# A graph layer with a residual and a norm: how the gathers of the prologue are held back

## The chip, the cores and the metric

One core of one Trainium2 chip runs the whole program. The metric is the device time of one execution in microseconds (us). Times are given as the median of several timed runs; a profile is one further execution, with a time of its own. TensorE is the matrix engine (PE in the profile, its weight loads PEld), VectorE is DVE, ScalarE is ACT, GpSimd is POOL, and SyncE (SP) issues most DMAs. GpSimd issues the indirect DMAs (the gathers) in this kernel.

## What is computed

A graph attention layer over N = 6250 nodes of 64 features and 206,250 edges sorted by destination, four heads of 16, with a residual and a layer norm:

```python
Qh = (x @ Wq.T + bq).reshape(n, H, D)
Kh = (x @ Wk.T + bk).reshape(n, H, D)
Vh = (x @ Wv.T + bv).reshape(n, H, D)
Ee = (edge_attr @ We.T + be).reshape(-1, H, D)
...
score = (Kh[src] * Qh[dst] * (1.0 / np.sqrt(D)) * Ee).sum(-1)
score = jnp.exp(jnp.clip(score, -5.0, 5.0))
msg = Vh[src] * score[..., None]
wV = jax.ops.segment_sum(msg, dst, num_segments=n)
...
x = _layernorm(x + wV.reshape(n, H * D))
```

So each edge needs k and v of its source node, q of its destination, and its own edge values; messages are summed by destination.

## The kernel before

The edges are cut into tiles of 128 and groups of G = 8 tiles (202 groups). Two groups make a step, except for the last eight groups, which are steps of their own. k and v of a step's sources lie in one of five buffers `kvs`, step s in `kvs[s % 5]`.

The prologue (lines 259 to 534) makes two tables in DRAM, `kv_tab` with k and v of every node and `q3_tab` with q cut into three bf16 parts. The loop of line 416 runs over five chunks of ten blocks of 128 nodes; TensorE multiplies two blocks at a time (line 424, a pair of products in one PSUM tile, 25 pairs), ScalarE copies k and v out (line 426) and takes the first part of q, VectorE the rest, and SyncE writes each chunk to the tables (lines 454 and 456). Between the pairs VectorE also works out masks, keys and the least destination of each group. SyncE then reads key rows, sources and edge values back for the first groups of the main part (lines 473 to 479).

Gathers from `kv_tab` cannot begin before the table is written. So the first two steps (groups 0 to 3, 32 tiles) get their k and v another way: GpSimd gathers rows of x itself, which is an input (line 318, `collect`), into the last of the five buffers, one gather a tile, 128 rows. Later TensorE turns them (`x_turned`, line 481), ScalarE copies the turned tiles, TensorE multiplies by the weights of k and v (line 494) and VectorE adds the bias and writes k and v into `kvs[0]` and `kvs[1]` (line 496). This goes by half groups, the eight entries of `order`; the loop of line 514 does one each time, and the turning of the next one is issued ahead of the product of this one. Between them stand ScalarE's and VectorE's pieces of work on x in three bf16 parts (`parts_of_x`) and ScalarE's one-hot rows (`onehot_rows`).

Steps 2 and 3 (groups 4 to 7) are the first whose k and v come from `kv_tab`. Their gathers are the eight lots of `lots(2) + lots(3)`, four gathers each, three in the last two (two tiles of every odd group from 7 on are picked by TensorE instead). `gather` (line 252) issues a lot.

Every engine works through its instructions in the order of the program. `behind` adds a wait by hand: a gather issued with it starts only when the named instruction is done. `mark` is a list of TensorE's instructions to wait for; before, these are the products of the tables and the first products of k and v. Nothing else orders GpSimd in the prologue except the data: src_x for gathers of x, the written `kv_tab` and src_i for those of k and v, and readers of a buffer that is overwritten.

Before, 8 gathers of x are issued at once and six lots of 4 follow in the loop of line 416, at the pairs 1, 4, 7, 10, 13 and 16; the first gather of each lot waits for the newest product. In the loop of line 514 each lot of steps 2 and 3 waits for the product of the same round:

```python
            first_kv(*gh, xe)
            xe = following
            gather(((lots(2) + lots(3))[i], mark[-1]))
```

The main part (from line 546, in a branch on a number that the prologue works out) loops over the 202 groups. In each, TensorE selects queries and node rows with one-hot matrices, turns terms and sums messages; VectorE makes the products (line 666), scores and messages; GpSimd issues the gathers of four steps ahead, each lot behind a TensorE instruction named in `where`.

Of the kernel before, what the change touches and what calls it, by code (L numbers as in the profile page):

```python
# [14 lines left out]
P = 128  # L15
N = 6250
C = 64
# [4 lines left out]
G = 8  # L22
# [18 lines left out]
XG = 4  # L41
# [63 lines left out]
def tile_gnn(ctx: ExitStack, tc: tile.TileContext, x, xT, wT, bias, beT, weT, eT, src, src_rows, dst,  # L105
             dst_rows, out):
    nc = tc.nc
# [48 lines left out]
    wkv = consts.tile([P, 2, 2 * C], F32, name="wkv")  # L156
# [102 lines left out]
    with tc.tile_pool(name="nodes", bufs=1) as nodes, \  # L259
# [49 lines left out]

        x_rows = kvs[KVB - 1].rearrange("p t (u c) -> p (t u) c", u=2)  # L310
        XS = [x_rows[:, g * G:(g + 1) * G, :] for g in range(XG)]
        first_lots = [(g, range(j, j + G // 2)) for g in range(XG) for j in (0, G // 2)]
        mark = []

        def collect(lot):
            g, js = lot
            for j in js:
                ins = nc.gpsimd.indirect_dma_start(
                    out=XS[g][:, j, :], out_offset=None, in_=x[:, :],
                    in_offset=bass.IndirectOffsetOnAxis(ap=src_x[:, g * G + j:g * G + j + 1], axis=0))  # L320
                if mark and j == js[0]:
                    behind(ins, mark[-1])

        collect(first_lots[0])
        collect(first_lots[1])


        nc.vector.tensor_scalar(ident, diff, 0.0, None, op0=OP.is_equal)
# [87 lines left out]
        for i in range(NB // CB):  # L416
            bs = slice(i * CB, (i + 1) * CB)
            kv_sb = chunks.tile([P, CB, 2 * C], F32, name="kv_sb")
            for b in range(0, CB, 2):
                two = slice(i * CB + b, i * CB + b + 2)  # L420
                ps = npsum.tile([P, 2, 3 * C], F32, name="ps")
                for u in range(2):
                    c0 = (i * CB + b + u) * P
                    mark.append(nc.tensor.matmul(ps[:, u, :], xT_sb[:, c0:c0 + P], w_sb, start=True,  # L424
                                                 stop=True))
                nc.scalar.activation(kv_sb[:, b:b + 2, :], ps[:, :, :2 * C], AF.Copy)
                q = ps[:, :, 2 * C:]
                nc.scalar.activation(q3[:, two, 0], q, AF.Copy)
                nc.vector.tensor_sub(q, q, q3[:, two, 0])
                late.append((q, two))  # L430
                if len(late) > 1:
                    rest_of_q()
                place = i, b
                if place == (0, 4):
                    for some in x_nodes:
                        nc.vector.memset(some[3 * P // 4:], 0.0)
                if place == (2, 0):
                    three_parts(be_p, be_sb, C, G)
                if place == (2, 4):
                    nc.vector.tensor_reduce(most, rows_i, axis=AX.X, op=OP.max)  # L440
                if place == (2, 8):
                    nc.vector.tensor_reduce(least, rows_i, axis=AX.X, op=OP.min)
                if place == (3, 0):
                    weights()
                if place == (3, 4):
                    three_parts(bkv_p, bkv_sb, 2 * C, 2)
                if place == (3, 8):
                    wide, one = destinations()
                if place == (4, 4):
                    masks()  # L450
                pair = (i * CB + b) // 2
                if pair % 3 == 1 and pair // 3 + 2 < len(first_lots):
                    collect(first_lots[pair // 3 + 2])
            nc.sync.dma_start(kv_v[:, bs, :], kv_sb)
            if i:
                nc.sync.dma_start(q3_v[:, bs.start - CB:bs.start], q3[:, bs.start - CB:bs.start])
            if i == 0:
                nc.sync.dma_start(rows_i, dst_rows)
            if i == 1:
                nc.sync.dma_start(src_i, src)  # L460
                nc.sync.dma_start(x_nodes[0][:N // NB], by_rows[:, :30 * C])
            if i == 2:
                nc.sync.dma_start(x_nodes[1][:N // NB], by_rows[:, 30 * C:])
                nc.sync.dma_start(dst_i, dst)
# [26 lines left out]
        def first_kv(g, h, xe):  # L491
            pv = npsum.tile([P, 4, 2 * C], F32, name="pv", bufs=2)
            for u in range(2):
                mark.append(nc.tensor.matmul(pv[:, 2 * u:2 * u + 2, :], xe[:, u, :], wkv, start=True,
                                             stop=True))
            nc.vector.tensor_add(kv_of(g)[:, 4 * h:4 * h + 4, :], pv,
                                 bkv_all[:, None, :].to_broadcast([P, 4, 2 * C]))

        def parts_of_x(i, part):

# [12 lines left out]
            parts_of_x(k, 0)  # L513
        for i, gh in enumerate(order):
            following = x_turned(*order[i + 1]) if i + 1 < len(order) else None
            first_kv(*gh, xe)
            xe = following
            gather(((lots(2) + lots(3))[i], mark[-1]))
            if i < 3:
                parts_of_x(i, 1)  # L520
                parts_of_x(i, 2)
# [7 lines left out]
            if i % 2:  # L529
                onehot_rows(i // 2, early_to[i // 2])  # L530
                onehot_rows_rest(i // 2)
        for b in range(RING):
            nc.sync.dma_start(acc[:, b, :], x[b * P:(b + 1) * P, :])
        later.close()
# [537 lines left out]
```

## Time and profile before

| | us |
|---|---|
| median of 3 timed runs | 2184.07 |
| lowest and highest of them | 2179.05, 2185.28 |
| profiled execution, its own time | 2166.65 |
| span of its profile | 2164.4 |
| busy in it: TensorE | 1896.9 |
| VectorE | 1212.6 |
| ScalarE | 881.3 |
| GpSimd | 1354.4 |

A row of the timeline has the start, the length, the engine, the line, the operation, output and inputs, and the shape; in brackets stands how long the engine had been idle and what ended that by the profile. Neighbouring instructions of one line and tile are merged, with their count behind an x. A tile is named by its buffer, so the gathers of x, which go into a `kvs` buffer, show as `kv<-in_x,src_x` and those of k and v as `kv<-kv_tab,src_i`. "issue" and "remote" are idle times that no event in the profile explains. A q behind an engine's name means its sequencer. Ends of matrix products are modelled, and some of their records can be missing.

### The profile page before, as it was taken

How to read it: one execution, taken by the hardware profiler on the slowest of the kernel's cores; microseconds unless marked ns; L12 is line 12 of the kernel's file. 1: busy time of each engine (PE TensorE's matmuls, PEld its weight loads, DVE VectorE, ACT ScalarE, POOL GpSimd, SP SyncE). 2: the span in 40 equal slices, each digit the busy share in tenths (PEclk: the TensorE clock that was granted, in tenths of full speed). 3: DMA queues.
4: the chain of work that ended last, by engine and by line, in shares of the span. 5: the costliest groups of instructions: out<-in, count | busy, mean ns of one | idle time of the engine just before them, and what ended most of it. 6: DMA issues, size and time to landing. Idle time of an engine off the chain costs nothing.

```text
span 2164.4 us, 26225 instructions
## 1 busy us (share of the span) xinstructions
PE 1896.9 (88%) x9156; PEld 1116.6 (52%) x9156; DVE 1212.6 (56%) x2179; ACT 881.3 (41%) x1166; POOL 1354.4 (63%) x1426
## 2 busy tenths in 40 slices
PE   6489999899888989899889889889898889989996
PEld 5245555455454555455455455555554545545555
DVE  6356556555555465665555555565655655655664
ACT  3343443443443434434434434434444344344343
POOL 5556666666666666666666666666666666666441
PEclk9688889888999889889989988988999988988995
DMA  6533343443343334434334433433433333333231
GB/s 179 185 96 92 108 110 96 112 110 97 111 114 92 105 98 118 113 97 114 106 96 115 111 90 110 116 90 110 113 103 111 97 110 110 95 111 109 83 90 25
DMA packets 141160, 230.01 MB, mean 106 GB/s; under 512 B 71056, under 2 KB 71506, under 8 KB 140906
## 3 DMA queue, kind: packets, MB, share of 16 engines
q1 hardware_dynamic: 95322, 135.39, 21.3%
q0 software_dynamic: 45312, 91.84, 16.8%
q8 instruction: 74, 1.21, 0.2%
q10 hardware_dynamic: 384, 1.00, 0.2%
q14 instruction: 68, 0.56, 0.1%
HBM read 220.31 MB, written 7.79 MB: 105 GB/s over the span
## 4 chain that ended last, share of the span: by engine, by line
PE 79%; issue 12%; DVE 3%; ACT 3%; another core or an unknown queue 2%; DMA 1%; SPq 0%; DVEq 0%; POOL 0%; ACTq 0%
PE pick L621 37%; PE room L621 24%; PE ee L621 11%; PE qe L650 4%; PE qq L621 3%; ACT off L693 1%; ACT to L224 1%; ACT to L218 1%; PE ps L424 1%; DMA kb<-key_tab 0%; ACT eb L632 0%; DVE hot L585 0%; DVE prod L666 0%; DVE score L669 0%
## 5 line engine op out<-in xcount | busy, mean ns | idle before, releaser
L235 POOL DMA_INDIRECT kv<-kv_tab,src_i x1384 | 1322.7, 956 | 750.3 <-issue 359.5
L621 PE MATMUL pick<-hot,parts 128*128 128x512 bf16 x3675 | 911.7, 405 | 16.3 <-issue 15.5
L621 PEld LDWEIGHTS <-parts 128*128 128x128 bf16 x3675 | 383.1, 105 | 561.8 <-issue 225.5
L645 DVE TENSOR_TENSOR term<-eb,qq 128x512 f32<-128x512 f32 x202 | 138.2, 684 | 757.3 <-remote 201.2
L621 PE MATMUL room<-msg,off 128*128 128x64 f32 x3192 | 462.3, 306 | 72.3 <-issue 69.6
L621 PEld LDWEIGHTS room<-msg,off 128*128 128x128 f32 x3192 | 438.6, 220 | 103.1 <-issue 99.9
L585 DVE TENSOR_TENSOR hot<-from,still 128x1536 bf16<-128x1536 bf16 (+1 forms) x384 | 375.7, 978 | 0.0
L621 PE MATMUL ee<-et,we_sb 128*128 128x512 f32 x404 | 274.1, 765 | 114.0 <-issue 86.1
L616 ACT ACTIVATE kv<-room 128x256 f32<-128x256 f32 x98 | 37.7, 384 | 819.3 <-DVE acc L719 542.9
L224 ACT ACTIVATE to<-to,one_p 126x1024 bf16<-126x1024 bf16 x198 | 226.9, 1146 | 6.4
L218 ACT ACTIVATE to<-kb,minus_row 126x1024 bf16<-126x1024 bf16 x198 | 224.8, 1135 | 0.0
L693 ACT ACTIVATE off<-of 128x2048 f32<-128x2048 bf16 (+2 forms) x105 | 191.5, 1825 | 6.9 <-DVE of L658 6.9
L675 ACT ACTIVATE score<-score 128x32 f32<-128x32 f32 x202 | 44.7, 221 | 357.9 <-DVE score L671 190.4
L632 ACT ACTIVATE eb<-ee,be_col 128x512 f32<-128x512 f32 x202 | 135.1, 669 | 29.5 <-DMA kb<-key_tab 22.4
L621 PEld LDWEIGHTS ee<-et,we_sb 128*128 128x128 f32 x404 | 73.9, 228 | 141.0 <-issue 108.2
L682 DVE TENSOR_TENSOR msg<-kv,score 128x512 f32<-128x512 f32 x202 | 137.8, 682 | 8.4 <-PE room L621 7.4
L669 DVE TENSOR_REDUCE score<-prod 128x32 f32<-128x512 f32 x202 | 138.3, 684 | 7.0
L666 DVE TENSOR_TENSOR prod<-kv,qe 128x512 f32<-128x512 f32 x202 | 137.2, 679 | 6.4 <-ACT kv L616 1.4
L658 DVE TENSOR_TENSOR of<-still,key 128x2048 bf16<-128x2048 bf16 (+2 forms) x105 | 123.1, 1173 | 7.0 <-ACT off L693 6.5
L650 PE MATMUL qe<-ident,term 128*128 128x128 f32 x806 | 123.3, 276 | 4.2 <-DVE term L645 2.1
L650 PEld LDWEIGHTS qe<-ident,term 128*128 128x128 f32 x806 | 101.9, 143 | 44.1 <-issue 3.7
L719 DVE SCALAR_TENSOR_TENSOR acc<-room,above,acc 128x64 f32<-128x64 f32 x101 | 28.5, 283 | 97.3 <-PE room L621 28.6
(124 smaller groups left out, 758.9 us busy)
## 6 DMA issues: line engine op xcount, KB each, us to landing
et<-in_eT SPq DMA_DIRECT2D x100, 512.0 KB
kb<-key_tab SPq DMA_DIRECT2D x201, 252.0 KB
kv<-kv_tab,src_i POOLq DMA_INDIRECT x1384
srcs<-in_src_rows SPq DMA_DIRECT2D x49, 256.0 KB
qw<-q_tab SPq DMA_DIRECT2D x202, 15.8 KB
kv_tab<-kv_sb SPq DMA_DIRECT2D x5, 640.0 KB
q_tab<-q SPq DMA_DIRECT2D x5, 480.0 KB
acc<-in_x SPq DMA_DIRECT2D x48, 32.0 KB
```

The source lines that it names most:

```text
L218: nc.scalar.activation(TO[g][:, :n, :], KB.pop(g)[:, :n * P].rearrange("p (j e) -> p j e", j=n), AF.Square, bias=minus_row3[:3 * W])
L224: nc.scalar.activation(TO[g][:, :n, :], TO[g][:, :n, :], AF.Relu, bias=one_p[:3 * W], scale=-1.0)
L235: return nc.gpsimd.indirect_dma_start(out=kv_of(g)[:, j, :], out_offset=None, in_=kv_tab[:, :], in_offset=bass.IndirectOffsetOnAxis(ap=src ...
L585: nc.vector.tensor_tensor(HOT[m, c][:, :hi - lo].rearrange("p b (a c) -> p b a c", c=2), pairs(FROM[m])[:, None].to_broadcast(shape), bloc ...
L621: mark.append(nc.tensor.matmul(*aps, **kw))
L632: nc.scalar.activation(EB[g][:, :n], ee[:, :n], AF.Identity, bias=be_col)
L645: nc.vector.tensor_mul(TERM[g][:, :n], EB.pop(g)[:, :n], qq[:, :n])
L650: nc.tensor.transpose(qe[g % 2][:, 2 * u:2 * u + 2, :].rearrange("p j c -> p (j c)"), TERM[g][:, u, :], ident)
L666: nc.vector.tensor_mul(prod[:, :n, :], kv_of(g)[:, :n, :C], qe[g % 2][:, :n, :])
L669: nc.vector.tensor_reduce(score, prod[:, :n, :].rearrange("p g (h d) -> p g h d", h=H), axis=AX.X, op=OP.add)
L682: nc.vector.tensor_mul(MSG[s][:, k:k + n, :].rearrange("p g (h d) -> p g h d", h=H), kv_of(g)[:, :n, C:].rearrange("p g (h d) -> p g h d", ...
L693: nc.scalar.activation(OF[s][:, :n, :], OH.pop(s)[:, :n, :], AF.Copy)
```

## The change

The gathers of x after the first eight are no longer issued in lots. `collect` issues one gather, and from the first pair of table products on, each pair is followed by one gather that waits for that pair's newest product, until all 32 are out (24 gathers, pairs 0 to 23). In the loop of the first k and v, `first_kv` no longer appends its products to `mark` but returns VectorE's addition, and a lot of steps 2 and 3 waits for that addition. The lots come one round later: in round i, from 1 on, lot i - 1 is issued behind addition i, and the last lot after the loop, behind addition 7 as well.

```diff
-        first_lots = [(g, range(j, j + G // 2)) for g in range(XG) for j in (0, G // 2)]
+        first_tiles = [(g, j) for g in range(XG) for j in range(G)]
         mark = []
 
-        def collect(lot):
-            g, js = lot
-            for j in js:
-                ins = nc.gpsimd.indirect_dma_start(
-                    out=XS[g][:, j, :], out_offset=None, in_=x[:, :],
-                    in_offset=bass.IndirectOffsetOnAxis(ap=src_x[:, g * G + j:g * G + j + 1], axis=0))
-                if mark and j == js[0]:
-                    behind(ins, mark[-1])
-
-        collect(first_lots[0])
-        collect(first_lots[1])
+        def collect(g, j):
+            ins = nc.gpsimd.indirect_dma_start(
+                out=XS[g][:, j, :], out_offset=None, in_=x[:, :],
+                in_offset=bass.IndirectOffsetOnAxis(ap=src_x[:, g * G + j:g * G + j + 1], axis=0))
+            if mark:
+                behind(ins, mark[-1])
+
+        for _ in range(G):
+            collect(*first_tiles.pop(0))
...
                 pair = (i * CB + b) // 2
-                if pair % 3 == 1 and pair // 3 + 2 < len(first_lots):
-                    collect(first_lots[pair // 3 + 2])
+                if first_tiles:
+                    collect(*first_tiles.pop(0))
...
             for u in range(2):
-                mark.append(nc.tensor.matmul(pv[:, 2 * u:2 * u + 2, :], xe[:, u, :], wkv, start=True,
-                                             stop=True))
-            nc.vector.tensor_add(kv_of(g)[:, 4 * h:4 * h + 4, :], pv,
-                                 bkv_all[:, None, :].to_broadcast([P, 4, 2 * C]))
+                nc.tensor.matmul(pv[:, 2 * u:2 * u + 2, :], xe[:, u, :], wkv, start=True, stop=True)
+            return nc.vector.tensor_add(kv_of(g)[:, 4 * h:4 * h + 4, :], pv,
+                                        bkv_all[:, None, :].to_broadcast([P, 4, 2 * C]))
...
-            first_kv(*gh, xe)
+            added = first_kv(*gh, xe)
             xe = following
-            gather(((lots(2) + lots(3))[i], mark[-1]))
+            if i:
+                gather(((lots(2) + lots(3))[i - 1], added))
...
+        gather(((lots(2) + lots(3))[-1], added))
         for b in range(RING):
```

## The prediction, on record before the changed kernel ran

> **What bounds the kernel now.** I read the page first: its span and the chain of work that ended last, by engine.
>
> ```profile
> span 2164.4 us, 26225 instructions
> ...
> PE 79%; issue 12%; DVE 3%; ACT 3%; another core or an unknown queue 2%; DMA 1%; SPq 0%; DVEq 0%; POOL 0%; ACTq 0%
> ```
>
> TensorE holds 79% of the chain and GpSimd 0% of it. The change edits GpSimd gathers of the prologue alone, so it can act only through who waits for them, or through the DMA engines. Next I read the group of the main loop's first VectorE product (one a group of edges), which shows how long the loop lasts.
>
> ```profile
> L666 DVE TENSOR_TENSOR prod<-kv,qe x202: 413/679/689, 112.5 to 2151.0; 128x512 f32<-128x512 f32 x101
> ```
>
> It comes 202 times between 112.5 and 2151.0 us: (2151.0 - 112.5) / 201 = 10.14 us a group. So about 112 us are prologue and entry, the part that the change can move; the loop behind it is not edited. Third, the timeline of the prologue's end: VectorE's additions 1 to 7 of the first k and v (numbered from 0), TensorE's last product for them, and TensorE's first instruction of the main part.
>
> ```profile
> 62.54 0.68 DVE L496 TENSOR_TENSOR kv<-pv,bkv_all 128x512 f32<-128x512 f32 x1
> 63.87 0.68 DVE L496 TENSOR_TENSOR kv<-pv,bkv_all 128x512 f32<-128x512 f32 x1
> ...
> 71.38 0.69 DVE L496 TENSOR_TENSOR kv<-pv,bkv_all 128x512 f32<-128x512 f32 x1 [0.69 <-issue]
> ...
> 75.37 0.67 DVE L496 TENSOR_TENSOR kv<-pv,bkv_all 128x512 f32<-128x512 f32 x1
> ...
> 79.70 0.68 DVE L496 TENSOR_TENSOR kv<-pv,bkv_all 128x512 f32<-128x512 f32 x1
> ...
> 81.74 2.08 PE L494 MATMUL pv<-wkv,xe 128*128 128x256 f32 x4 [0.41 <-ACT xe L488]
> ...
> 90.16 0.69 DVE L496 TENSOR_TENSOR kv<-pv,bkv_all 128x512 f32<-128x512 f32 x1 [9.78 <-remote]
> 99.25 0.69 DVE L496 TENSOR_TENSOR kv<-pv,bkv_all 128x512 f32<-128x512 f32 x1 [8.40 <-remote]
> 100.00 0.10 PEld L556 LDWEIGHTS <-row_b 128*128 128x128 bf16 x1 [16.91 <-DVE kv L496]
> ```
>
> The last addition ends at 99.25 + 0.69 = 99.94 and the main part starts at 100.00: this addition, not a gather, ends the prologue. Its product is on record as done at 81.74 + 2.08 = 83.82, so the last two additions came 8.4 to 9.8 us later than the recorded inputs explain, and the profile has no name for the releaser ("remote"). I call these about 15 us the gap (99.25 - 83.82 = 15.4). Every rival below turns on it or on what starts behind it.
>
> **The change, first part: gathers of x.** Before, 8 gathers go at once and 24 follow in six lots of 4, each lot held by the newest product of the tables. After, the same 8 go at once and each of the other 24 is held by one product pair, pairs 0 to 23. I read when a pair is done from ScalarE's copy behind it, which starts at once; these are the 15th, 16th, 22nd and 24th of the 25 copies.
>
> ```profile
> 39.28 0.38 ACT L426 ACTIVATE kv_sb<-ps 128x256 f32<-128x256 f32 x1 [3.78 <-remote]
> ...
> 44.29 0.38 ACT L426 ACTIVATE kv_sb<-ps 128x256 f32<-128x256 f32 x1 [4.29 <-issue]
> ...
> 53.02 0.38 ACT L426 ACTIVATE kv_sb<-ps 128x256 f32<-128x256 f32 x1 [0.51 <-PE ps L424]
> ...
> 55.58 0.38 ACT L426 ACTIVATE kv_sb<-ps 128x256 f32<-128x256 f32 x1 [0.56 <-PE ps L424]
> ```
>
> ```profile
> 41.04 0.94 POOL L318 DMA_INDIRECT kv<-in_x,src_x  x1 [0.30 <-issue]
> ...
> 48.28 0.95 POOL L318 DMA_INDIRECT kv<-in_x,src_x  x1 [0.30 <-issue]
> 64.05 0.94 POOL L235 DMA_INDIRECT kv<-kv_tab,src_i  x1 [14.82 <-DMA kb<-key_tab]
> ```
>
> The last x gather moves from 48.28 to about 55.6, and ends at 56.5. Behind it on GpSimd stands the first gather of k and v, which starts at 64.05 only: 7.5 us of cover remain. The last x tiles are read by the transposes of the eighth half group, which sit ahead of the product at 81.74, some 20 us after the gather: covered too. More waits cost GpSimd's sequencer a row each, at most 18 more of 17 ns (the row of these waits below), 0.3 us inside the same cover. If the cover were gone, each microsecond would be one for GpSimd, not for TensorE.
>
> What does move is DMA traffic. By 44.2 us the kernel before has issued 28 x gathers (8 and five lots, the last row 41.04); after, 8 + 15 = 23. Five leave the stretch from 20 to 44; three, those of pairs 21 to 23, now fall behind 53.0, into the stretch where the key rows are written and read back.
>
> ```profile
> L318 POOLq EVENT_SEMAPHORE  x6: 17/17/17, 12.0 to 39.8; - x6
> ```
>
> ```profile
> q0 software_dynamic: 1024, 1.05, 9.9%
> ```
>
> That is the gathers' queue from 0 to 60 us: 1024 packets in 9.9% of 16 engines, so 0.099 x 16 x 60 / 1024 = 0.093 us a packet, 32 packets a gather, 32 x 0.093 / 16 = 0.19 us of all engines. Five are worth 0.95 us, three 0.56 us.
>
> ```profile
> 40.00:50.00 10.00, 4.76 (x13) 3.67 (x13) 7.46 (x29) 3.49 (x16) 5.45 (x6) 1.00 0.83 264
> 50.00:60.00 10.00, 9.55 (x30) 8.41 (x31) 7.68 (x33) 6.00 (x21) 0.00 (x0) 1.00 0.74 282
> 60.00:70.00 10.00, 3.94 (x18) 2.86 (x17) 4.68 (x8) 5.36 (x10) 4.71 (x5) 0.87 0.96 306
> 80.00:90.00 10.00, 3.40 (x8) 1.69 (x6) 0.38 (x1) 3.84 (x5) 7.56 (x9) 0.50 0.18 46
> 90.00:100.00 10.00, 0.00 (x0) 0.00 (x1) 1.38 (x2) 0.00 (x0) 6.76 (x8) 0.50 0.21 52
> 100.00:110.00 10.00, 5.71 (x12) 1.75 (x13) 0.79 (x2) 1.38 (x2) 2.32 (x3) 0.50 0.80 238
> ```
>
> The columns are busy time of PE, PEld, DVE, ACT and POOL, then the granted clock, the DMA share and GB/s. I weigh traffic by the share of the stretch that it enters or leaves. Leaving the stretch up to 44 (0.83 where it ends) gives between 0 (nothing there waits for a load by name) and -0.95 us; I take -0.8. Joining the one at 0.96, where ScalarE waits 4.6 us for the first key rows (next fence) with TensorE behind it, costs between 0 and 0.56; I take +0.5.
>
> ```profile
> 59.78 3.69 SPq L211 DMA_DIRECT2D kb<-key_tab  x4
> ...
> 66.61 1.15 ACT L218 ACTIVATE y<-kb,minus_row 126x1024 bf16<-126x1024 bf16 x1 [4.61 <-DMA kb<-key_tab]
> ```
>
> **Second part: gathers of k and v.** Lot i was held by product i, now by addition i + 1, the last by addition 7. The lots start 5.0 us apart from 64.05. Lots 0 to 4 start at 64.05, 69.04, 74.30, 79.29 and 84.66; their new holders end at 63.22, 64.55, 72.07, 76.04 and 80.38, from the rows above. Each is ahead, so these five lots do not move. The rest:
>
> ```profile
> 89.65 0.94 POOL L235 DMA_INDIRECT kv<-kv_tab,src_i  x1 [0.30 <-issue]
> ...
> 99.49 0.95 POOL L235 DMA_INDIRECT kv<-kv_tab,src_i  x1 [1.41 <-remote]
> ...
> 101.99 0.95 POOL L235 DMA_INDIRECT kv<-kv_tab,src_i  x1 [0.30 <-issue]
> 116.91 0.94 POOL L235 DMA_INDIRECT kv<-kv_tab,src_i  x1 [13.98 <-PE pick L621]
> ```
>
> Lot 5 waits for 90.85 instead of starting at 89.65 (1.2 us); lots 6 and 7, three gathers each, wait for 99.94, and at 1.25 us each the last ends at 107.4 instead of 102.9. Queued behind it on GpSimd are the main part's gathers, whose first starts at 116.91 after 14 idle us, released by TensorE: 9.5 us of cover remain. The data of these lots are for groups 6 and 7, whose products come six groups of 10.14 us after 112.5. So nobody is late, as long as TensorE does not come to its first products over 9 us sooner.
>
> Again only traffic moves: three gathers that ran before 100 now run between 100 and 107.4, beside the loads with which the main part starts (DMA share 0.80). From 100.5 to 110 us the queue shows
>
> ```profile
> q0 software_dynamic: 96, 0.20, 12.2%
> ```
>
> so 0.122 x 16 x 9.5 / 96 = 0.19 us a packet, 0.39 us a gather, 1.16 us for three: between 0 and 1.16, and I take 0.80 of it, +0.9.
>
> The sum is -0.8 + 0.5 + 0.9 = **+0.6 us**, with ends at -0.95 and +1.7. The profiled execution took 2166.65 us, its span 2164.4 and 2.25 around it; it would become 2167.3. The median of the three timed runs is 2184.07, 17.4 above it, which no row splits up, so I carry the difference over as it is: 2184.7.
>
> **Weighing a rule.** From 77.6 to 111.7 us TensorE's granted clock is half, behind that whole:
>
> ```profile
> 77.60:111.70 34.10, 12.40 (x28) 5.25 (x26) 5.85 (x9) 7.03 (x9) 18.44 (x20) 0.50 0.39 110
> 111.70:142.40 30.70, 26.15 (x123) 12.94 (x122) 20.38 (x31) 17.14 (x21) 18.66 (x20) 1.00 0.28 76
> ```
>
> So the entry runs at half clock, and a later entry can stay there longer. The Trainium skill (TensorE: Matmul & The Clock Gate, Part 1) has the clock change only at the edges of a free-running window of about 3.4 us, after one busy or one idle window; 34.1 is ten of these, so the trace agrees, and by that rule a slip of 0.6 us costs either nothing or, where it crosses an edge, one window at half rate. By it the sum would be 0.6 or, as an estimate from that page, up to 2.3.
>
> **The rivals.** *Faster: the gap closes.* If the gap came from gathers running beside the last products, spacing them could let additions 6 and 7 start at 81.3 and 83.8: 15.4 us less, 2168.7. For it: in the gap GpSimd and its queue alone work (80 to 100 us above). Against: up to lot 4, that is until 88, the same gathers run at the same times; DMA is at 0.18 to 0.21, and the additions at 71.38 to 79.70 passed beside the same stream. A smaller gain of the same sign, the 4.6 us wait for key rows, stays inside 0.3%.
>
> *Slower: the entry slips.* The six held gathers start at 99.94, 0.06 us before the main part's own loads. If they go ahead of these in the engines' rings, the first terms wait for all six, 6 x 0.39 = 2.3 us, at half clock; the half-clock stretch then lasts one piece of the trace longer (6.8 us, a fifth of the 34.1), in which TensorE does half its work, another 3.4; with the upper end of the key rows' 0.56 and half a group's pause the loop may have to make up again, some 8 us: 2192. It decides as soon as the held gathers' packets stand ahead of the first loads. Against: GpSimd needs 1.25 us a gather, so at most two are ahead.
>
> *The change does nothing at the places it names:* five of eight lots start as before. That is my forecast, within an error of 2 us. *The loop's rhythm shifts:* the loop repeats 10.14 us a group from where it is entered, and a different entry could cost or save a few of them: plus or minus 7 to 10 us, either sign, seen nowhere in one trace.
>
> **How the numbers follow.** Forecast, all covered: 0.46, 2184.7. Gap closes: 0.15. Entry slips: 0.22. Rhythm: 0.17, of which 0.10 slower and 0.07 faster. So faster by over 0.3% (6.6 us, about what a measurement of this kernel can tell from no change) 0.22, within 0.46, slower 0.32. The likeliest case alone runs from 2181 to 2188 (the sum's ends and the spread of the timed runs); the range goes on to the gap's 2169 and, past 2192, to 2196 for a shifted rhythm.
>
> **What would show it.** Right: the last x gather at about 55.6; lots 0 to 4 within 1 us of the starts above; the last prologue gather ending near 107; the last addition near 99; the first L666 near 113. Wrong: additions 6 and 7 right behind their products (gap closed); the first term or the first key rows later by over 2 us (entry slips); the first L666 in place but the last one moved by over 5 us (rhythm). A GpSimd gather at the head of a wait of TensorE or VectorE in the loop's first eight groups would break the cover that I counted on.

## The result, and the profile after

| | before | after |
|---|---|---|
| median of 22 runs each, us | 2182.47 | 2176.82 |
| lowest and highest | 2174.93, 2185.91 | 2168.11, 2185.57 |
| profiled execution's own time | 2166.65 | 2185.57 |

The ratio is 0.9976 with a 95% interval of 0.9965 to 0.9987: the changed kernel is about 5 us faster. The forecast was +0.6 us. The two profiled executions say the opposite of the medians, since single executions of one kernel lie 11 to 17 us apart; from here on a profile tells where something happens, and only timed runs tell how long the whole takes.

The page of the changed kernel, and the group of the main loop's first VectorE product (line 665 now):

```profile
span 2183.3 us, 26096 instructions
...
PE 69%; issue 15%; ACT 7%; DVE 4%; another core or an unknown queue 2%; POOL 1%; DMA 1%; DVEq 0%; ACTq 0%; POOLq 0%; SPq 0%
```

```profile
L665 DVE TENSOR_TENSOR prod<-kv,qe x202: 414/680/690, 109.7 to 2170.0; 128x512 f32<-128x512 f32 x101
```

The loop is entered 2.8 us sooner (109.7, before 112.5) and ends 19 us later, in an execution that is not the median. Next the timeline at the prologue's end, additions 4 to 7 (line 493) with the last products (line 492) and TensorE's first instruction of the main part:

```profile
75.29 0.67 DVE L493 TENSOR_TENSOR kv<-pv,bkv_all 128x512 f32<-128x512 f32 x1
...
79.16 2.08 PE L492 MATMUL pv<-wkv,xe 128*128 128x256 f32 x4
79.61 0.68 DVE L493 TENSOR_TENSOR kv<-pv,bkv_all 128x512 f32<-128x512 f32 x1
...
82.85 2.08 PE L492 MATMUL pv<-wkv,xe 128*128 128x256 f32 x4 [1.61 <-issue]
...
90.14 0.69 DVE L493 TENSOR_TENSOR kv<-pv,bkv_all 128x512 f32<-128x512 f32 x1 [9.84 <-remote]
...
92.27 0.69 DVE L493 TENSOR_TENSOR kv<-pv,bkv_all 128x512 f32<-128x512 f32 x1 [1.45 <-remote]
...
93.02 0.29 PE L555 MATMUL still<-ident_b,row_b 128*128 128x128 bf16 x1 [8.10 <-DVE kv L493]
```

Addition 6 stands where it stood (90.14, before 90.16). Addition 7 comes 7.0 us sooner (92.27, before 99.25), and the main part with it (93.02, before 100.00). So of the prediction's gap, 15.4 us from the recorded end of the last product to addition 7, 7.3 us are left (82.85 + 2.08 = 84.93 to 92.27). GpSimd's timeline, at its last x gather, its first gather of k and v, and the lots that are held:

```profile
52.21 0.94 POOL L316 DMA_INDIRECT kv<-in_x,src_x  x1 [0.52 <-PE ps L422]
63.88 0.94 POOL L235 DMA_INDIRECT kv<-kv_tab,src_i  x1 [10.73 <-DMA kb<-key_tab]
...
88.31 0.94 POOL L235 DMA_INDIRECT kv<-kv_tab,src_i  x1 [0.30 <-issue]
91.09 0.94 POOL L235 DMA_INDIRECT kv<-kv_tab,src_i  x1 [1.84 <-issue]
...
102.32 0.94 POOL L235 DMA_INDIRECT kv<-kv_tab,src_i  x1 [0.30 <-issue]
114.23 0.94 POOL L235 DMA_INDIRECT kv<-kv_tab,src_i  x1 [10.97 <-PE pick L620]
```

Lots 0 to 4 run as before (63.88 to 88.31). Then GpSimd stands still for 1.84 us, from 89.25 until addition 6 is done. Addition 6 starts 0.9 us after GpSimd came to rest, and addition 7 follows 2.1 us behind it, where before it took 9.1. Whether the pause brought them one profile cannot tell; the experiments come back to it. ScalarE's last table copy in the kernel before (line 426), then the same copy (line 424) and ScalarE's first one-hot rows in the changed one:

```profile
56.86 0.38 ACT L426 ACTIVATE kv_sb<-ps 128x256 f32<-128x256 f32 x1 [0.56 <-PE ps L424]
```

```profile
53.25 0.38 ACT L424 ACTIVATE kv_sb<-ps 128x256 f32<-128x256 f32 x1 [0.56 <-issue]
...
66.52 1.15 ACT L218 ACTIVATE y<-kb,minus_row 126x1024 bf16<-126x1024 bf16 x1 [8.13 <-DMA kb<-key_tab]
```

The tables are done 3.6 us sooner (53.25, before 56.86), but ScalarE then waits 8.13 us for the key rows instead of 4.61, and goes on at the same time as before (66.52, before 66.61).

### The profile page after: what moved, and what is told of

It reads as the page before. It is cut to its first block, busy times and chain, and to the rows that moved or that the text cites. A ratio compares the mean times of both kernels' runs of the same rounds, so it can differ in the third digit from the quotient of the medians.

```text
span 2183.3 us, 26096 instructions
## 1 busy us (share of the span) xinstructions
PE 1875.8 (86%) x9010; PEld 1106.5 (51%) x9156; DVE 1214.9 (56%) x2179; ACT 881.0 (40%) x1166; POOL 1349.8 (62%) x1426
## 4 chain that ended last, share of the span: by engine, by line
PE 69%; issue 15%; ACT 7%; DVE 4%; another core or an unknown queue 2%; POOL 1%; DMA 1%; DVEq 0%; ACTq 0%; POOLq 0%; SPq 0%
PE pick L620 32%; PE room L620 21%; PE ee L620 10%; PE qe L649 4%; PE qq L620 3%; ACT off L692 2%; ACT to L224 1%; ACT to L218 1%; POOL kv L235 1%; ACT eb L631 1%; DVE prod L665 0%; DVE score L668 0%; DVE hot L584 0%; ACT kv L615 0%
## 5 line engine op out<-in xcount | busy, mean ns | idle before, releaser
L620 PE MATMUL pick<-hot,parts 128*128 128x512 bf16 x3529 | 884.0, 399 | 42.6 <-issue 37.3
L620 PEld LDWEIGHTS <-parts 128*128 128x128 bf16 x3675 | 377.7, 103 | 563.3 <-issue 227.0
L620 PE MATMUL room<-msg,off 128*128 128x64 f32 x3192 | 447.7, 302 | 51.3 <-issue 50.4
L620 PEld LDWEIGHTS room<-msg,off 128*128 128x128 f32 x3192 | 427.2, 216 | 80.2 <-issue 78.4
```

The source lines that it names most:

```text
L620: mark.append(nc.tensor.matmul(*aps, **kw))
```

## The experiments

The runs fell in five sets, and the sets differ in the TensorE clock that was granted over the span: 0.88 to 0.90 as in the first measurement in three of them (kernel before 2167 to 2187 us), 0.965 to 0.97 in two (kernel before 1837 to 1841 us). One chip gave both, in different sets. A ratio is always against the kernel before in the same set.

### Each part alone, and both kernels again, at 0.965

The x gathers one by one with the lots of before (`first_kv` and its loop as before):

> The first part alone: gathers of x one at a time behind each pair of table products, lots of k and v as before. Three theories of the 5.2 us (ratio 0.998) that the change saved. (A) The last lots of k and v: in the changed kernel's profile addition 6 comes at 90.14 and addition 7 at 92.27, against 90.16 and 99.25 before, because lots 5 to 7 now stand still until the additions. By A this kernel keeps the old gap, addition 7 near 99, first group's product near 112.5, ratio 1.000 within 0.001. (B) The x gathers: the table copies ended 3.6 us sooner in the changed kernel's profile (last one 53.25, before 56.86). By B this kernel has the gain, ratio 0.997 to 0.998, with the last table copy near 53. (C) Neither: both are the luck of one execution and the gain comes from where the loop's rhythm is entered; then this kernel's ratio can lie anywhere from 0.997 to 1.003 and doesn't follow the time of its addition 7.

The lots held by the additions, with x gathers in lots of four (`collect` and its calls as before):

> The second part alone: gathers of x in lots of four as before, lots of k and v held by the additions one round later. By A (the lots of k and v make the gain) the ratio is 0.997 to 0.998, addition 7 is within 3 us of addition 6 (near 92) and the first group's product near 110. By B (the x gathers make it) the ratio is 1.000 within 0.001 and the last table copy near 57. By C (rhythm, no tie to either part) the ratio lies anywhere from 0.997 to 1.003.

The kernel before, and the changed one, unchanged:

> The kernel before, unchanged, for a second profile of it. By A the times of one execution are those of the kernel: addition 6 near 90, addition 7 near 99, the last table copy near 57. By C they move from execution to execution by several microseconds: the 9 us between additions 6 and 7 may be gone here.

> The changed kernel, unchanged, timed again and with a second profile. By A and B the ratio is 0.9965 to 0.9987 again and addition 7 comes within 3 us of addition 6. By C its profile may show the 9 us between additions 6 and 7 again, and the ratio may go back to 1.000.

Measured: x part 1.0000 (0.9990 to 1.0009), k and v part 0.9998 (0.9988 to 1.0009), both 1.0004 (0.9995 to 1.0013). Nothing moves. The profile of the kernel before in this set, products 6 and 7 and their additions:

```profile
74.01 2.08 PE L494 MATMUL pv<-wkv,xe 128*128 128x256 f32 x4 [0.69 <-ACT xe L488]
...
76.13 0.69 DVE L496 TENSOR_TENSOR kv<-pv,bkv_all 128x512 f32<-128x512 f32 x1 [0.98 <-PE pv L494]
...
76.50 2.08 PE L494 MATMUL pv<-wkv,xe 128*128 128x256 f32 x4 [0.41 <-ACT xe L488]
...
78.61 0.69 DVE L496 TENSOR_TENSOR kv<-pv,bkv_all 128x512 f32<-128x512 f32 x1 [1.79 <-PE pv L494]
```

Each addition starts 2.1 us behind the start of its product, and the profile names TensorE, not "remote". There is no gap here, although the gathers stream as before, from 59.0 us on. Nor does it come later: TensorE is busy in at least 9.95 of every 10 us from 90 to 130. So the kernel's order of work alone does not make the gap; it shows only in the sets with the lower granted clock.

### Each part alone at 0.88

The same two kernels and the kernel before, in another set:

> The first part alone once more (x gathers one at a time, lots of k and v as before), for a chip whose granted clock is near 0.88; the first four runs fell on one at 0.965, where neither part nor both moved the time. Theory A (lots of k and v): at 0.88 the ratio is 1.000 within 0.0015. Theory B (x gathers): 0.997 to 0.998 with the last table copy near 53. Theory C (the clock decides, not a part: what the change gains it gains through how TensorE's throttled windows fall in one execution): ratio between 0.997 and 1.003, not tied to addition 7. If the clock is 0.965 again: 1.000 within 0.001 by all three.

> The second part alone once more (lots of k and v held by the additions). At a clock near 0.88: by A 0.997 to 0.998 with addition 7 within 3 us of addition 6; by B 1.000 within 0.0015; by C between 0.997 and 1.003. At 0.965: 1.000 within 0.001 by all.

> The kernel before, unchanged, for one more profile. At a clock near 0.88, by A the 9 us between additions 6 and 7 stand again; by C the stretch from the last product's record to addition 7 may be anything between 0 and 15 us. At 0.965 the additions come 2 to 3 us apart, as in the last profile of it (76.13, 78.61).

and later the changed kernel, the k and v part once more, and the kernel before with each lot one round later but still behind a product:

```diff
-            gather(((lots(2) + lots(3))[i], mark[-1]))
+            if i:
+                gather(((lots(2) + lots(3))[i - 1], mark[-1]))
...
+        gather(((lots(2) + lots(3))[-1], mark[-1]))
```

> The changed kernel once more, for a chip near 0.88. If the 0.24% belong to the kernel on such a chip: ratio 0.9965 to 0.9987. If the two parts, each alone 1.000 and 0.999 there, only add up: 0.999 within 0.0015. If the clock is near 0.965, where the gathers of k and v run from the prologue to the end almost without a pause, the three to four microseconds by which the last lots are held back can only cost: 1.000 to 1.002.

> The second part alone again (lots of k and v held by the additions, x gathers in lots of four). Near 0.88 its first run gave 0.9988 (0.997 to 1.0005), and the whole change twice 0.9976. If this part carries the gain: 0.9965 to 0.9990 again, with addition 7 between 90 and 96. If both parts are needed: 0.9990 to 1.000. Near 0.965: 1.000 to 1.002.

> The kernel before with each lot of k and v one round later but still held by a product, not by an addition; the x gathers in lots of four as before. If what counts is that the stream stops a lot or two earlier for the last products (H), this does it as well as the additions do: addition 7 near 90 to 95 instead of 97 to 101, ratio 0.9965 to 0.999 near 0.88. If it is the kind of holder, ratio 1.000 within 0.0015 and addition 7 near 99. Near 0.965: 1.000 to 1.002.

Measured, with the times read from the timelines (us); the third column is from the start of product 7 on record to the start of addition 7:

| kernel | ratio to before | product 7 to addition 7 | addition 7 | main part | first product of the loop |
|---|---|---|---|---|---|
| before | | 17.5 | 99.25 | 100.00 | 112.5 |
| before again | | 8.7 | 96.96 | 97.71 | 109.0 |
| x part | 1.0002 (0.9988 to 1.0015) | 18.5 | 100.55 | 101.29 | 111.7 |
| changed | 0.9976 (0.9965 to 0.9987) | 9.4 | 92.27 | 93.02 | 109.7 |
| changed again | 0.9976 (0.9957 to 0.9995) | 13.9 | 95.35 | 96.10 | 109.2 |
| k and v part | 0.9988 (0.9970 to 1.0005) | 7.4 | 90.52 | 91.27 | 110.7 |
| k and v part again | 1.0002 (0.9983 to 1.0021) | 8.7 | 94.22 | 94.97 | 103.4 |
| products, a round later | 0.9987 (0.9967 to 1.0006) | 10.1 | 92.99 | 93.74 | 109.0 |

The gain of the whole is there again. All three profiles with the old lots have addition 7 between 97 and 101, all five with the later lots between 90 and 96, products as holders as well as additions: the later round counts, not the kind of holder. On average the main part starts at 99.7 with the old lots and at 93.8 with the later ones, 5.9 us sooner. At the loop's first product 2.7 us are left (111.1 and 108.4), and half of these come from one profile: without the 103.4 the later lots average 109.7.

The timelines of GpSimd say what the later round does. A held lot makes GpSimd stand still, in a later round sooner. In seven of these eight profiles the addition that is due next then starts 0.9 to 2.7 us after GpSimd came to rest (which was between 88.9 and 98.1). But beside a stream without a rest TensorE crawls, it doesn't stand still: in three profiles addition 6 came late but while gathers still ran (88.35 to 91.45), and so did addition 7 in the profile of the k and v part, at 90.52, with no gather waiting over 0.31 us up to 102. So the next addition follows a rest, but additions also come without one, 7 to 12 us behind the one before.

The x part alone is worth nothing, as the wait for the key rows said. The k and v part's two ratios, weighted by their intervals, make 0.9994 with 0.0013 either way: less than the whole change's 0.9976 (0.0010). Parts multiplied give 0.9996 within 0.0019, 0.0020 from the whole, just inside what the intervals allow (0.0021). Whether the parts merely add up or help each other stays open. So does the cause of the 5 us in the total: that the later lots bring the end of the prologue forward is shown, but the kernels that have this without the x part gave 0.9988, 1.0002 and 0.9987, and no run ties the gain of the whole to it. Theory C, that where the loop is entered decides, is not excluded.

### What makes the gap

At 0.88 the additions are late while gathers stream, one behind the other. So first the changed kernel with all eight lots behind addition 7, and with lots 3 to 7 behind it:

```diff
-            if i:
-                gather(((lots(2) + lots(3))[i - 1], added))
...
-        gather(((lots(2) + lots(3))[-1], added))
+        for lot in lots(2) + lots(3):
+            gather((lot, added))
```

> The changed kernel with all eight lots of k and v held by addition 7, so that no gather runs beside the last products. By A additions 6 and 7 follow their products without the gap (near 81 and 84 at a clock of 0.88), and TensorE's main part starts 8 us sooner than in the changed kernel. By B and C the gap at 0.88 stays (additions near 90 and 92 to 99). The 30 gathers then run from about 80 (clock 0.965) or 93 (0.88) at 1.25 us each, so they end near 118 or 131; by the cover counted in the prediction groups 4 to 7 are needed four groups after the first product, 85 + 4 x 8.6 = 119 at 0.965 and 110 + 4 x 10.1 = 150 at 0.88: no cost at 0.88 and at most 2 us at 0.965.

```diff
-            if i:
+            if 1 <= i <= 3:
                 gather(((lots(2) + lots(3))[i - 1], added))
...
-        gather(((lots(2) + lots(3))[-1], added))
+        for lot in (lots(2) + lots(3))[3:]:
+            gather((lot, added))
```

> The changed kernel with lots 0 to 2 of k and v as they are and lots 3 to 7 all behind addition 7, so the stream of gathers stops near 79 and goes on when the last products of the prologue are done. Theory H (at a granted clock near 0.88 to 0.9 TensorE crawls while a stream of gathers has gone on for some 16 us, and gets on when it stops): additions 6 and 7 on time (near 81 and 83), main part from near 84, first product of VectorE near 92, then a second stream of 18 gathers from 84 to 107, with the crawl from about 100 in the first groups. With all lots last that stream had 30 gathers and the total was 1.005; without any it was 0.991; so here 0.996 to 1.002. Theory I (gathers don't matter): additions as in the changed kernel. Near 0.965, where the gathers are the bound: the stop of 3 to 5 us is lost, 1.002 to 1.003.

Then without these gathers, and with an iota (a GpSimd instruction that fills a tile with counted numbers) behind each:

```diff
+        def load_kv(g):
+            n = sum(len(js) for s in (2, 3) for h, js in lots(s) if h == g)
+            nc.sync.dma_start(kv_of(g)[:, :n, :],
+                              kv_tab[:P * n, :].rearrange("(p t) c -> p t c", t=n))
...
+        for g in (4, 5):
+            load_kv(g)
...
-            if i:
-                gather(((lots(2) + lots(3))[i - 1], added))
...
-        gather(((lots(2) + lots(3))[-1], added))
+        for g in (6, 7):
+            load_kv(g)
```

> The 30 gathers of steps 2 and 3 are left out; four plain loads by SyncE bring as many rows from the top of the table into the same tiles, so k and v of groups 4 to 7 are those of other nodes. Theory H (the stream): at a clock near 0.88 a stream of gathers, one behind the other for some 16 us, is what slows TensorE to a crawl (in the kernel before the gathers start at 64 and additions 6 and 7 are late from 80 on; with all lots last the gathers start at 84 and TensorE's products come 1.4 us apart instead of 0.23 from 102 on). By H additions 6 and 7 follow their products here (near 81 and 83.5), the main part starts near 84 and its first product of VectorE near 92, and no crawl comes before some 16 us after the main part's first gather. Theory I (TensorE's own work, or the time since the tables): the crawl comes near 80 to 105 as in the kernel before, gathers or not. At 0.965 neither shows, and the ratio is 1.000 within 0.003.

> The 30 gathers of steps 2 and 3 are left out (plain loads bring rows from the top of the table, so k and v of groups 4 to 7 are those of other nodes), for a chip near 0.88. By H (a stream of gathers of some 16 us slows TensorE to a crawl there) additions 6 and 7 follow their products (near 81 and 83.5), the first product of VectorE comes near 92, and TensorE crawls, if at all, some 16 us after the main part's first gather. By I (TensorE's own work or time) additions 6 and 7 are late as in the kernel before. At 0.965: ratio 0.997 as in the first run of it.

```diff
+        pause = nodes.tile([P, 1024], I32, name="pause")
+
+        def paced(lot):
+            (g, js), after = lot
+            for j in js:
+                ins = gather_kv(g, j)
+                if j == js[0]:
+                    behind(ins, after)
+                nc.gpsimd.iota(pause, pattern=[[1, 1024]], base=0, channel_multiplier=1)
...
-                gather(((lots(2) + lots(3))[i - 1], added))
+                paced(((lots(2) + lots(3))[i - 1], added))
...
-        gather(((lots(2) + lots(3))[-1], added))
+        paced(((lots(2) + lots(3))[-1], added))
```

> The changed kernel with an iota of 1024 elements a partition (about 1.3 us, from 0.32 us for 224) behind every gather of steps 2 and 3, so these come about 2.5 us apart instead of 1.25 and end near 140 instead of 103; their first readers stand four groups behind the first product, near 135 to 150. By H at a clock near 0.88 a stream at half the rate does not bring the crawl: additions 6 and 7 near 81 and 83.5, first product near 92, and up to 17 us of the total are saved, if no later stream takes it back. By I no difference in the prologue, and the gathers behind run 36 us late, which costs up to 10 us. At 0.965: 1.000 to 1.005.

> The changed kernel with an iota behind every gather of steps 2 and 3, which put them 2.1 us apart in its first run, for a chip near 0.88. By H at this rate no crawl: additions 6 and 7 near 81 and 83.5; by I as in the changed kernel, 90 and 92 or later. In its first run, at 0.968, the readers of group 4 waited for its gathers until 129, and all of the 36 us by which the gathers ended later were lost (1.020). At 0.88 the loop is entered 17 to 25 us later and GpSimd has 1.4 us a group to spare, so by H the total is 1.000 to 1.010, by I 1.005 to 1.015.

Measured near 0.88 to 0.90:

| kernel | ratio to before | product 7 to addition 7 | main part | first product of the loop |
|---|---|---|---|---|
| all lots last | 1.0049 (1.0030 to 1.0068) | 2.1 | 84.18 | 92.4 |
| lots 3 to 7 last | 0.9974 (0.9955 to 0.9993) | 2.1 | 84.42 | 92.9 |
| no gathers | 0.9914 (0.9888 to 0.9939) | 1.2 | 83.09 | 89.6 |
| iota behind each | 1.0102 (1.0078 to 1.0127) | 2.1 | 83.95 | 133.0 |

In all four the gap is gone. The iota put the gathers 2.1 us apart, not 2.5, and its addition 7 at 83.20 comes 19.9 us after its first gather. That is weak evidence on the rate, since at the full rate the k and v part (table above) had addition 6 within 1 us of its time 18.8 us after its first gather (83.44 and 64.64). Additions 6 and 7 without the gathers:

```profile
80.80 0.69 DVE L493 TENSOR_TENSOR kv<-pv,bkv_all 128x512 f32<-128x512 f32 x1 [0.98 <-PE pv L492]
...
82.34 0.69 DVE L493 TENSOR_TENSOR kv<-pv,bkv_all 128x512 f32<-128x512 f32 x1 [0.85 <-PE pv L492]
```

So theory H holds for the gap, and theory I falls. The same profile shows what H said of the gathers that are left: the main part's own begin at 92.91 and run one behind the other until 115.08. From about 113 TensorE's products stand over 2 us apart, and VectorE waits until 118.66:

```profile
110.95 2.24 PE L626 MATMUL pick<-hot,parts 128*128 128x512 bf16 x9
...
115.62 0.58 PE L626 MATMUL pick<-hot,parts 128*128 128x512 bf16 x1 [2.43 <-issue]
...
118.66 0.69 DVE L650 TENSOR_TENSOR term<-eb,qq 128x512 f32<-128x512 f32 x1 [8.71 <-remote]
```

But a gap that is closed is not a gain by itself. The table by stretches of the kernel with all lots last (columns as in the prediction: busy PE, PEld, DVE, ACT, POOL, then granted clock, DMA share, GB/s), and VectorE's first instruction after the stop:

```profile
90.00:100.00 10.00, 9.17 (x37) 3.95 (x39) 5.69 (x8) 5.86 (x7) 7.56 (x9) 1.00 0.66 206
100.00:110.00 10.00, 4.17 (x15) 1.20 (x13) 0.00 (x0) 0.00 (x0) 7.56 (x9) 0.79 0.19 51
110.00:120.00 10.00, 0.00 (x0) 0.00 (x0) 0.00 (x0) 0.00 (x0) 7.56 (x9) 0.50 0.21 52
120.00:130.00 10.00, 0.00 (x0) 0.00 (x0) 0.00 (x0) 0.00 (x0) 7.56 (x9) 0.50 0.21 54
```

```profile
135.92 0.69 DVE L643 TENSOR_TENSOR term<-eb,qq 128x512 f32<-128x512 f32 x1 [40.17 <-remote]
```

Its gathers, 30 of the lots and eight of the main part, stream from 84.39 to 131.5. TensorE works beside them until about 102, then hardly gets anything done until they stop, and VectorE stands idle for 40.17 us. The loss has moved out of the prologue, where TensorE had two products to do, into the loop, where it has whole groups. With the gathers split, the stop is 24 us (first product of the loop at 92.89, second at 116.49) and the total is the changed kernel's: no faster version, although the prologue ends 9 us sooner. Only without the gathers does most of the 20 us at the loop's start (89.6, changed kernel 109.2 in that set) come through: 16.0 us of the medians there (2147.93 and 2163.96). That kernel also issues 30 gathers fewer, and no run separates the two.

The totals with the iota tell nothing of the gathers: its scratch tile lies in memory that the main part's tiles take over, and ScalarE waited for it (second execution, 0.876):

```profile
126.83 0.69 ACT L641 ACTIVATE eb<-ee,be_col 128x512 f32<-128x512 f32 x1 [43.58 <-POOL pause L519]
```

That was a flaw of the experiment; its additions, 44 us ahead of that, stand.

### What the lots cost where there is no gap

The changed kernel again, and with lots 0 to 2 behind addition 3 as well, so that the gathers start 8 us later:

> The changed kernel unchanged, timed again, for a chip whose granted clock is near 0.88. If its 0.24% belong to the kernel the ratio is 0.9965 to 0.9987 again; the two parts alone gave 1.000 and 0.999 there, so if the parts only add up it is 0.999 within 0.0015. At a clock of 0.965 it is 1.000 within 0.001.

```diff
-            if i:
-                gather(((lots(2) + lots(3))[i - 1], added))
+            if i >= 3:
+                for lot in (lots(2) + lots(3))[i - 1 if i > 3 else 0:i]:
+                    gather((lot, added))
```

> The changed kernel with lots 0 to 2 of k and v held by addition 3 as well, so the gathers start near 72 instead of 64 and go on without a break. By H at a clock near 0.88 the crawl starts 8 us later, near 88: additions 6 and 7 on time (near 81 and 83.5), the main part starts near 84, and the crawl falls into its first products. By I the additions are as in the changed kernel, 6 near 90 and 7 near 92 to 99. Total by H: between the changed kernel and the one with all lots last (1.005), so 1.000 to 1.004; by I 0.998 to 1.000. At 0.965: 1.000 within 0.002.

Both fell in a set at 0.968: the changed kernel 1.0012 (1.0001 to 1.0023), gathers from addition 3 on 1.0055 (1.0034 to 1.0077), in the same set no gathers 0.9970 (0.9954 to 0.9986) and the iota behind each 1.0201 (1.0181 to 1.0221), with the flaw just named. Neither H nor I expected the cost of gathers from addition 3 on. GpSimd's gathers of k and v in the kernel before, first at 0.965, then in the profile of the prediction (count, ns, first and last start):

```profile
L235 POOL DMA_INDIRECT kv<-kv_tab,src_i x1384: 940/944/1476, 59.0 to 1813.4; - x198
```

```profile
L235 POOL DMA_INDIRECT kv<-kv_tab,src_i x1384: 938/944/1477, 64.1 to 2121.3; - x198
```

and who let it wait (total, times, longest), in the same order:

```profile
POOL kv L235 <- issue: 333.7, 1095, 0.3
...
POOL kv L235 <- PE pick L621: 12.8, 42, 0.3
```

```profile
POOL kv L235 <- PE room L621: 105.2, 48, 7.6
POOL kv L235 <- PE pick L621: 89.2, 40, 14.0
```

At 0.965 no gather behind the first ever waits longer than 0.3 us: 1384 of them go in one stream of 1754 us. VectorE's first product of a group waits for them 87 times there, 148.1 us in total; in the profile of the prediction no wait of VectorE's is put down to them. So at 0.965 the stream sets the end, and what holds it up is lost. With the gathers from addition 3 on it starts at 67.2 instead of 59.7 in the changed kernel, 7.5 us later, and the median is 9.7 us later (1848.52 and 1838.82):

```profile
L235 POOL DMA_INDIRECT kv<-kv_tab,src_i x1384: 940/944/1493, 67.2 to 1825.7; - x198
```

Without the gathers of steps 2 and 3 the stream starts 32.8 us later than in the kernel before (91.8 and 59.0) and is 30 gathers of 1.25 us shorter, 4.7 us less; its median fell by 5.5 (1831.63 and 1837.17).

The changed kernel's own hold shows in its sequencer's waits at 0.968, one of which lasts 3.5 us, but it does not reach the stream:

```profile
L235 POOLq EVENT_SEMAPHORE  x401: 17/17/3497, 56.1 to 1805.7; - x134
```

In the same profile no gather behind the first waits over 0.32 us up to 103, and the stream lasts 1753.5 us (59.66 to 1813.2), as in the kernel before. So the 1.7 us of its median (1838.82 and 1837.17) are not shown to come from the hold, and the other set near 0.965 had 1.0004.

## Why the prediction was wrong, point by point

- **Gathers of x.** Forecast: last one at 55.6, covered, DMA traffic worth -0.8 and +0.5. It came at 52.21, since the tables themselves were done 3.6 us sooner, which the sum did not have. The sign was in the prediction's own rows: two table copies had 3.78 and 4.29 us idle before them, while x gathers streamed. With single gathers such unexplained waits are gone (the longest left before a copy, 2.69 us, is for a write to the table), and in the sets near 0.88 the last copy is at 52.9 to 53.4 with single gathers and at 56.9 to 58.0 with lots. The key rows swallow it, so the value, nothing, was right (x part alone 1.0002), but by luck: 3.6 us won and 3.5 us lost are not the -0.8 and +0.5 of the sum.
- **Lots 0 to 4 do not move.** Right: they start within 0.2 us of before, from 63.88 on.
- **Lots 5 to 7.** Lot 5 at 91.09 was forecast (90.85). The last gather ended at 103.26 and not at 107.4, because its holder, addition 7, came 7 us sooner than the forecast took for granted.
- **"Again only traffic moves."** This step failed. It let the gathers of lots 5 to 7 act only on DMA, priced at +0.9 us, and took the gap as fixed, so that addition 7 had to come near 99. At a granted clock near 0.88 they act on TensorE: it crawls beside a long stream, the gap is gone where the stream is moved or left out (2.1 and 1.2 us from product 7 to addition 7), and with the lots a round later addition 7 came at 90.5 to 95.4. The argument against the rival *gap closes* was that the same gathers run up to 88 and that earlier additions passed beside the same stream. The first is true, but addition 7 lies behind 88, where the lots do differ. That addition 6 stood at 90.14 and 90.16 is chance: with the same gathers up to 88 it lies between 83.4 and 96.2 in the eight profiles. The second fails because a stream has to last some time first: 16 us in the kernel before (first gather 64.05, addition 5 at 79.70 the last on time).
- **The rival** *gap closes* had the right mechanism and too large a size: 15.4 us at the end of the prologue, where 7.0 came in this profile and 5.9 on average, and it had the main part keep all of it, where 2.7 are left at the loop's first product. The median fell by 5.7 us, and how much of that is the gap's no run shows.
- *Entry slips* did not happen. Its 8 us did not follow from its rows either: 2.3, 3.4 and 0.56 are 6.3, and the pause of half a group had no figure. *Rhythm shifts* was given a sign that proves nothing: the loop, from its first product to its last, took 2038.5 and 2054.8 us in two profiles of the kernel before.
- **Granted clock.** The prediction weighed the half clock as the price of the entry. It isn't what slows TensorE there. In the profile of the kernel before at 0.966 the stretch from 60 to 90 us was granted 0.56 to 0.71, and there was no gap. In the split kernel TensorE all but stops while the granted clock is 0.90:

```profile
100.00:110.00 10.00, 4.37 (x17) 1.57 (x16) 0.00 (x0) 0.00 (x0) 7.56 (x9) 0.90 0.21 52
```

From 103 to 108 it is 1.00 there, and single products stand 1.4 and 2.1 us apart (104.50, 105.90 and 108.00).

The Trainium skill's rule (TensorE: Matmul & The Clock Gate, Part 1) of windows of about 3.4 us fits the recorded edges, whose stretches stay multiples of 3.41 us (6.8, 3.4, 34.1 and 30.7 in the profile of the prediction), but has nothing that would bring this stop.

## What to carry to other kernels

When an engine's results come late without a releaser in the profile, look at what another engine streams meanwhile, and ask what stops the stream: here a hold on GpSimd's gathers moved the end of the prologue by when it paused them, not by what it ordered. Ask of a stall where it will go when it is driven out: here it cost less in a prologue in which TensorE has little to do (0.9976) than in the loop (1.0049). And ask what bounds the kernel when TensorE is throttled less: the change that gave 0.9976 at a clock near 0.88 gave no gain at 0.965 and 0.968 (1.0004 and 1.0012), where the stream of gathers sets the end and a start 7.5 us later cost 9.7.

## What the runs showed of the hardware

Two regimes for one program: on one and the same chip the kernel before took 1837 us at a granted clock of 0.969 and 2167 at 0.892 in another set. In the first, gathers stream for 1754 us beside TensorE without such a stop. In the second, 16 to 20 us of gathers at 1.25 us each (first gather and onset: before 64.05 and some 80; all lots last 84.39 and 102; split 84.63 and 103; no gathers of steps 2 and 3 92.91 and 113) bring TensorE nearly to a stop that the granted clock does not show. In the loop it ends some 4 us after the stream does (all lots last: 131.5 and 135.92; split: 111.8 and 115.89, the next VectorE terms), at the prologue's end 0.9 to 2.7 us after it. TensorE's records in the split kernel show the onset:

```profile
100.06 2.97 PE L621 MATMUL pick<-hot,parts 128*128 128x512 bf16 x13
104.50 0.38 PE L621 MATMUL pick<-hot,parts 128*128 128x512 bf16 x1 [1.47 <-issue]
105.90 0.38 PE L621 MATMUL pick<-hot,parts 128*128 128x512 bf16 x1 [1.02 <-issue]
108.00 0.58 PE L621 MATMUL pick<-hot,parts 128*128 128x512 bf16 x1 [1.73 <-issue]
```

Thirteen products in 2.97 us, 0.23 us each, then single ones 1.4 us apart and more. With the gathers 2.1 us apart it had not come at 84 us, which is little beyond the onsets above. What in the chip does this (power, or something that TensorE and the gathers share) no run here shows, nor why a set of runs falls into one regime or the other. The Trainium skill (TensorE: Matmul & The Clock Gate, Part 1) warns that recorded clock events can be unreliable and the gate has been seen stuck at a quarter for over 50 us; a step to a sixth (an estimate, 0.23 us against 1.4), which this trace does not list, would be of that kind, but that is argued and not shown.
